# Row maxima of three attentions: from products over 128 rows, one head at a time, to products over 64 rows, two heads side by side

## The chip, the cores and the metric

The program runs on one NeuronCore of a Trainium2 chip. The core has a matrix engine (TensorE, "PE" in the profile, with "PEld" for its weight loads), three engines for elementwise work (VectorE "DVE", ScalarE "ACT", GpSimd "POOL"), and a queue engine (SyncE, "SP") that issues most transfers between the device's memory and the core's own memory (SBUF). Matrix products land in a small accumulator memory, PSUM, which DVE and ACT read. Each engine runs its own instructions in order; they wait for one another through semaphores.

The metric is the time of one execution on the device in microseconds (us). Three runs of the kernel before took 3617.41, 3617.8 and 3612.1 us; the median is 3617.41.

## The reference, cut to what matters

The program is four blocks on an input of 4 batches, 1024 positions and 128 channels. Each block normalizes x, computes an attention-like part s and a gate g from it, and adds s * g:

```
xn = _layernorm(x, axis=-1)
s = _L0_attn_ref(xn, ...)          # block 0: 16 heads of 8, window of 250, causal
g = _silu(_L0_ffn_ref(xn, ...))
x = x + s * g
```

Blocks 0, 1 and 2 hold attentions with 16 heads of dimension 8. They differ in which keys a query sees:

```
mask = (delta >= 0) & (delta < CONTEXT)   # block 0 ("window"), CONTEXT = 250
mask = jnp.tril(...)                      # block 1 ("causal")
                                          # block 2 ("full"): no mask
scores = jnp.einsum('bhtd,bhsd->bhts', q, k) * D ** (-0.5)
attn = jax.nn.softmax(scores, axis=-1)
x = jnp.einsum('bhts,bhsd->bhtd', attn, v)
```

Around them run a channel mix (block 0), a mixture of experts for all tokens (block 1), a feed-forward layer and a mixture of experts with limited places (block 2). Block 3 is a state-space layer with two layers of local attention; the change doesn't touch it.

## The kernel before, in words

**Products of parts.** q and k are computed in float32 and split into three bfloat16 parts each (`_split`, line 166), so that a float32 product becomes nine bfloat16 products of parts. With a head dimension of 8, the nine products take 72 rows of the contraction: `q9` holds the three parts of q three times over, `k9` each part of k three times (rows 0 to 71). Rows 72 to 74 of `q9` hold the three parts of the negative row maximum, and `k9` is 1 there: a product over all 128 rows is then the score less its row's maximum. The rest is zero against one.

**Units.** A unit is one batch with four of its sixteen heads: 16 units in each of the three attentions, in the order of `order` (line 516). For each unit, `load` (line 278) fetches `q9` and `k9` from the device's memory, where `project` had stored the parts (`store`, line 245): three transfers of 24 rows for q (L285), nine of 8 rows for k (L288), and, from the fourth unit on, one of zeros into rows 72 to 74 (L290), because the buffers go round and the maxima are computed with the same tile before the rows of maxima are filled. There are three pairs of buffers.

**Maxima.** `maxima(n)` (line 293) makes steps for unit n. A step takes a PSUM tile `max_ps` of two banks of 512 columns (two such tiles in rotation, shared with others), fills it with products of 128 queries of a head with the keys that they see (L317), adds the mask by a product of the identity with a mask tile (L333) for each head, and reduces it on DVE with a negated maximum (L344) into `neg`. There are 14 steps to a unit in the window stage, 22 in the causal one, 32 in the full one. `split` turns the maxima into three parts on POOL; `spread` transposes them on PE (`neg_ps`), copies them on DVE and stores them into rows 72 to 74 of `q9` by three transfers (L371, `negr`).

**Weights.** `attend(n)` (line 397) computes, for each block of keys, the transposed scores less the maxima (`sc`, L410, lhsT from `k9`, rhs from `q9`), their exponentials on ACT (L417), in blocks with a mask a select on POOL (L387), and the products with the values into `o_ps` (L438), in four column tiles of 32. In steps, `first` does two heads' scores, `second` the values of an earlier block and the other two heads' scores. There are 40 scores to a unit in the window stage, 48 in the causal one and 64 in the full one.

**Order.** `rest` (line 524) goes through the units: beside the weights of unit n run the remaining steps of the maxima of n + 1, their split, the first steps of n + 2 (two fifths of them, `lead`), and the spread of n + 1. At the start of unit n, `load(n + 2)` is issued. The streams are interleaved evenly by `_interleave` (line 174), with the projections of the next batch and parts of the neighbouring blocks among them.

```
ahead = steps[lead:] + ending[:1]
last = ending[1]
if n + 2 < N:
    load(n + 2)
    steps, ending = maxima(n + 2)
    ahead += steps[: lead - 2] + [last] + steps[lead - 2 : lead]
```

PE's instructions stay in the order in which the program records them (`keep_in_program_order`). The order on other queues, SP's among them, is set by a planner when the program is built: an instruction without a pin can stand earlier or later than in the text.

Of the kernel before, what the change touches and what calls it, by code (L numbers as in the profile page):

```python
# [185 lines left out]
def _attention(k, pool, mode, xT, w, out, rope=None):  # L186
# [9 lines left out]

    nc = k.nc
    scale = HD**-0.5
    dense = {}
    units = {}  # L200
    place = 16 * ("window", "causal", "full").index(mode)
# [76 lines left out]
    def load(n):  # L278

        b, g = order[n]  # L280
        q9, k9 = k.q9[(place + n) % 3], k.k9[(place + n) % 3]
# [7 lines left out]
        if place + n > 2:  # L289
            nc.sync.dma_start(q9[72:75].rearrange("p h t -> p (h t)"), k.zeros)  # L290
        units[n] = (q9, k9)

    def maxima(n):
# [3 lines left out]
        def tile_of(parts):  # L297


            def step():  # L300
                q9, k9 = units[n]
                if "neg" not in held:
                    held["neg"] = pool.tile([P, 4, NT], F32, tag="neg", name="neg", bufs=3)
                neg = held["neg"]
                ps = ps2("max_ps")
                flat = ps.rearrange("p a c -> p (a c)")
                _, qt0, _ = parts[0]
                lo = max(0, qt0 - 2) * P if mode == "window" else 0
                hi = T if mode == "full" else (qt0 + 1) * P
                width = hi - lo  # L310
                for j, qt, place in parts:
                    lhs = q9[:, j, qt * P : qt * P + P]
                    for c0 in range(lo, hi, 512):
                        c1 = min(c0 + 512, hi)
                        at = place + c0 - lo
                        masked = mode != "full" and c1 == hi
                        matmul(  # L317
                            flat[:, at : at + c1 - c0],
                            lhsT=lhs,
                            rhs=k9[:, j, c0:c1],  # L320
                            start=True,
                            stop=not masked,
                            skip_group_check=True,
                        )
                        if masked:
                            mw = min(c1 - c0, k.mask[mode].shape[1])

                            W = k.mask[mode].shape[1]
                            spans = [(W - P, W)]
                            if W - mw < W - CONTEXT:  # L330
                                spans.insert(0, (W - mw, W - CONTEXT))
                            for m0, m1 in spans:
                                matmul(  # L333
                                    flat[:, at + c1 - c0 - W + m0 : at + c1 - c0 - W + m1],
                                    lhsT=k.ident16,
                                    rhs=k.mask[mode][:, m0:m1],
                                    start=False,
                                    stop=m1 == W,
                                    skip_group_check=True,
                                )  # L340
                j0, m = parts[0][0], len(parts)
                stride = parts[1][2] - parts[0][2] if m > 1 else width
                of = flat[:, 0 : m * stride].rearrange("p (n c) -> p n c", n=m)[:, :, 0:width]
                nc.vector.tensor_reduce(neg[:, j0 : j0 + m, qt0], of, AX.X, ALU.max, negate=True)  # L344

            return step

        steps = []
        for qt in range(NT):
# [4 lines left out]
            for j in range(0, 4, per):  # L354
                steps.append(tile_of([(j + i, qt, i * pitch) for i in range(per)]))
# [1689 lines left out]
```

## Time and profile before

One execution was profiled. It took 3610.66 us; the span from its first to its last instruction is 3608.9 us, at a mean granted clock of TensorE of 0.951.

| what | value |
|---|---|
| the profiled execution's own time | 3610.66 us |
| its span | 3608.9 us |
| median of the three runs | 3617.41 us |
| PE busy | 3138.7 us, 87% |
| DVE busy | 2445.6 us, 68% |
| ACT busy | 1988.7 us, 55% |
| POOL busy | 1417.2 us, 39% |
| products into max_ps, masks not counted | 2198 recorded, 625.0 us busy |
| reductions of max_ps on DVE | 1088, 1177.9 us busy |
| scores of the weights on PE | 2403 recorded, 651.8 us busy |
| loads of q9 / of k9 / of zeros | 144 / 432 / 45 transfers |

How to read it: "busy" is the time in which an engine has an instruction in work, and products on PE are pipelined, so that one product's time is longer than its distance from the next; distances are read from the timeline's start times. In a line of groups stand the source line, the engine and operation, the tile written and the tiles read, the shapes, the count, the busy time, the mean duration of one in ns, and the idle time of the engine before them with what ended it. A PE shape such as 128\*128 is rows by columns of the array that the product uses. In a line of the timeline stand start and length in us, the engine, the same names and a count of merged instructions; the bracket is the engine's idle time before it and what ended it. In the trace, the window stage of block 0 lies roughly between 100 and 500 us, the causal stage of block 1 between 800 and 1300, the full stage of block 2 between 1520 and 2430, and block 3 after 2500.

### The profile page before, as it was taken

The numbers are of one execution on the slowest core, as the hardware profiler recorded it, in microseconds if no ns is written. First come the engines' busy times: TensorE is split into PE (matmuls) and PEld (weight loads), VectorE is DVE, ScalarE is ACT, GpSimd is POOL, SyncE is SP. The second block draws the span as 40 slices with busy tenths as digits, with TensorE's granted clock in tenths as the row PEclk, the third lists the DMA queues.
The fourth block names the chain that finished last, engine by engine and source line by source line (L and its number), as shares of the span: only waits on it lengthen the run. The fifth ranks groups of instructions, "written<-read, shape, count | busy, mean of one in ns | idle before, by whom it ended". The sixth has DMA issues, their size and how long they took to land. (4 is left out here: it accounts for less than half of the span.)

```text
span 3608.9 us, 64740 instructions
## 1 busy us (share of the span) xinstructions
PE 3138.7 (87%) x24592; PEld 1704.4 (47%) x24729; DVE 2445.6 (68%) x4927; ACT 1988.7 (55%) x4191; POOL 1417.2 (39%) x1962
## 2 busy tenths in 40 slices
PE   4889889999898986899999989677499999989897
PEld 3545446654343433433323333223366666666665
DVE  7667664457777752788786766652587888778785
ACT  2444453346555552366665665554366666666674
POOL 5555552012323223030321300211576667656663
PEclk8999999999999997999999999888699999999999
DMA  3322312112222102011111221100210111010110
GB/s 99 71 60 55 70 42 83 46 33 51 57 42 57 34 22 69 21 44 28 41 34 33 55 53 31 33 19 9 78 22 18 21 25 24 18 25 22 29 26 21
DMA packets 133083, 146.09 MB, mean 40 GB/s; under 512 B 80403, under 2 KB 107931, under 8 KB 125467
## 3 DMA queue, kind: packets, MB, share of 16 engines
q1 hardware_dynamic: 130724, 137.75, 16.0%
q0 software_dynamic: 2048, 4.20, 0.4%
q8 instruction: 196, 3.21, 0.4%
q14 instruction: 115, 0.93, 0.1%
HBM read 93.83 MB, written 30.11 MB: 34 GB/s over the span
## 5 line engine op out<-in xcount | busy, mean ns | idle before, releaser
L417 ACT ACTIVATE pt<-sc 128x512 f32<-128x512 f32 (+3 forms) x2432 | 1077.0, 511 | 786.1 <-PE sc L78 737.7
L344 DVE TENSOR_REDUCE neg<-max_ps 128x1 f32<-128x1024 f32 (+6 forms) x1088 | 1177.9, 1102 | 477.2 <-PE max_ps L78 424.1
L78 PE MATMUL sc<-q,k 128*128 128x512 bf16 (+3 forms) x2403 | 651.8, 342 | 126.2 <-ACT pt L417 70.0
L78 PE MATMUL max_ps<-k,q 128*128 128x512 bf16 (+3 forms) x2198 | 625.0, 350 | 86.2 <-DVE neg L344 39.5
L78 PE MATMUL o_ps<-pt,va 128*32 128x512 f32 (+3 forms) x4864 | 560.6, 527 | 19.9 <-POOL pt L387 10.2
L387 POOL TENSOR_SCALAR_AFFINE_SELECT pt<-pt 128x256 f32<-128x256 f32 (+2 forms) x768 | 292.3, 399 | 568.2 <-ACT pt L417 566.3
L78 PEld LDWEIGHTS <-k 128*128 128x128 bf16 x2432 | 183.0, 98 | 544.2 <-issue 418.1
L78 PEld LDWEIGHTS <-q 128*128 128x128 bf16 x2304 | 222.7, 99 | 359.6 <-issue 241.2
L168 POOL CAST negp<-neg 128x32 bf16<-128x32 f32 x48 | 10.2, 212 | 719.3 <-DVE neg L344 719.2
L1603 ACT ACTIVATE pr<-lsc,nb,r 128x128 f32<-128x128 f32 x512 | 202.7, 476 | 61.2 <-DVE nb L1595 57.6
L1524 POOL TENSOR_TENSOR qn<-qn,rot 128x512 f32<-128x512 f32 x128 | 164.9, 1294 | 139.8 <-DVE rot L1516 125.9
L1533 POOL TENSOR_TENSOR rn<-ss,neghalf 128x16 f32<-128x16 f32 x64 | 188.9, 2951 | 68.8 <-DVE ss L1531 59.3
L78 PEld LDWEIGHTS o_ps<-pt,va 128*32 128x32 f32 x4864 | 99.7, 109 | 213.8 <-issue 160.3
L691 ACT ACTIVATE h<-hp,eb 128x512 f32<-128x512 f32 x128 | 80.9, 684 | 197.8 <-PE hp L78 190.2
L78 PEld LDWEIGHTS <-ident 128*128 128x128 bf16 x1472 | 146.2, 100 | 87.5 <-issue 22.7
L1441 PE MATMUL qk_ps<-wqkv,hT 128*128 128x512 f32 x256 | 137.9, 623 | 24.9 <-DVE hT L1487 10.3
L78 PE MATMUL hp<-xT,ew 128*128 128x512 f32 x256 | 130.3, 634 | 19.7 <-ACT rope_t L234 9.3
L701 DVE SCALAR_TENSOR_TENSOR xn<-op,gates,xn 128x128 f32<-128x128 f32 x256 | 72.1, 344 | 100.4 <-PE op L78 100.4
L78 PEld LDWEIGHTS op<-ew,h 128*128 128x128 f32 x1024 | 123.6, 192 | 20.1 <-issue 17.0
L78 PE MATMUL max_ps<-mask_window,ident 128*128 128x134 bf16 (+2 forms) x960 | 132.0, 221 | 0.0
L78 PE MATMUL op<-ew,h 128*128 128x128 f32 x1024 | 125.3, 276 | 0.0
L65 POOL TENSOR_TENSOR ln_rs<-ln_ve,neghalf 128x4 f32<-128x4 f32 x72 | 73.7, 1025 | 113.1 <-DVE ln_ve L63 109.7
(347 smaller groups left out, 5452.9 us busy)
## 6 DMA issues: line engine op xcount, KB each, us to landing
q<-qx SPq DMA_DIRECT2D x144, 192.0 KB
k<-kx SPq DMA_DIRECT2D x432, 64.0 KB
va<-vb SPq DMA_DIRECT2D x120, 128.0 KB
x<-x SPq DMA_DIRECT2D x20, 512.0 KB
qx<-qp SPq DMA_DIRECT2D x12, 768.0 KB
kx<-kp SPq DMA_DIRECT2D x12, 768.0 KB
ew<-in_e1w_dram SPq DMA_DIRECT2D x64, 128.0 KB
x<-in_x_dram SPq DMA_DIRECT2D x8, 512.0 KB
```

The source lines that it names most:

```text
L65: nc.gpsimd.tensor_tensor(rs, ve, k.neghalf[:, :n], ALU.pow)
L78: k.tc.keep_in_program_order(k.nc.tensor.matmul(*args, **kw))
L168: eng.tensor_copy(dst[:, 0], src)
L344: nc.vector.tensor_reduce(neg[:, j0 : j0 + m, qt0], of, AX.X, ALU.max, negate=True)
L387: nc.gpsimd.affine_select(out=pt, in_=pt, pattern=[[0, 2], [step, pt.shape[2]]], compare_op=ALU.is_ge, fill=0.0, base=base, channel_multip ...
L417: nc.scalar.activation(pt[:, j % 2, :width], sc[:, :width], AF.Exp, scale=scale)
L691: nc.scalar.activation(h[:, hh, :], hp[:, hh, :], AF.Gelu, bias=eb1[:, e, hh : hh + 1])
L701: nc.vector.scalar_tensor_tensor(to, op[:, c, :], gates[:, 4 * n + c, e : e + 1], to, ALU.mult, ALU.add)
L1441: pin(nc.tensor.matmul(*args, **kw))
L1524: nc.gpsimd.tensor_tensor(qn[:, i], qn[:, i], rot, ALU.add)
L1533: nc.gpsimd.tensor_tensor(rn, ss.rearrange("p w h -> p (w h)"), k.neghalf[:, : 2 * NH], ALU.pow)
L1603: nc.scalar.activation(t.pr[:, h, :], t.sc[r][:, c, :], AF.Exp, bias=t.nb[r][:, c : c + 1], scale=t.r8[:, h : h + 1])
```

## The change

Maxima get their own operands. `load_pairs` fetches, for a unit, tiles `q8` and `k8` of 128 rows by two heads: rows 0 to 63 hold two heads of the unit, rows 64 to 127 the other two. Eight products of parts are kept (the one of the two lowest parts is left out), which fill 64 rows. A product over 64 rows then takes half of the array, and products for the two halves are recorded one behind the other, each into its own bank of the PSUM tile. The weights keep `q9` and `k9` with nine products over 128 rows.

The masks are added once per bank: one product of the identity over 128 rows with the mask repeated for all places of the bank, before the products where the mask covers a whole block of 128 keys, after them where it covers six columns. For this, window and causal maxima are taken block of keys by block of keys: the diagonal block, the one before it and the one before that in the window stage; the diagonal block, keys up to 512 and keys from 512 on in the causal one; the two halves of the keys in the full one. Each part has its own `neg`; `split` first takes the minimum of the parts on DVE.

`load(n + 1)` is now issued at the start of unit n, with two pairs of buffers in place of three, and after it `load_pairs(n + 2)`, also with two. The zeros fall away. The steps of a unit are 11, 20 and 32.

```
-        q9, k9 = k.q9[(place + n) % 3], k.k9[(place + n) % 3]
+        q9, k9 = k.q9[n % 2], k.k9[n % 2]
...
-        if place + n > 2:
-            nc.sync.dma_start(q9[72:75].rearrange("p h t -> p (h t)"), k.zeros)
...
+    def load_pairs(n):
+        b, g = order[n]
+        q8 = pool.tile([P, 2, T], BF16, tag="q8", name="q8", bufs=2)
+        k8 = pool.tile([P, 2, T], BF16, tag="k8", name="k8", bufs=2)
+        for a in range(2):
+            heads = slice(4 * g + 2 * a, 4 * g + 2 * a + 2)
+            for r in range(3):
+                r0, ns = 64 * a + 24 * r, 3 if r < 2 else 2
+                nc.sync.dma_start(q8[r0 : r0 + 8 * ns], dense["q", b][0 : 8 * ns, heads, :])
+                for s in range(ns):
+                    nc.sync.dma_start(k8[r0 + 8 * s : r0 + 8 * s + 8], dense["k", b][8 * r : 8 * r + 8, heads, :])
+        pairs[n] = q8, k8
...
+                def mask(first):
+                    m0, m1 = masked
+                    m = k.mask[mode][:, m0:m1].unsqueeze(1).to_broadcast([P, len(slots), m1 - m0])
+                    for a in range(2):
+                        to = ps[:, a, 0 : len(slots) * pitch].rearrange("p (n c) -> p n c", c=pitch)
+                        matmul(
+                            to[:, :, 0 : m1 - m0], lhsT=k.ident16, rhs=m, start=first, stop=not first, skip_group_check=True
+                        )
+                whole = masked is not None and masked[1] - masked[0] == P
+                if whole:
+                    mask(True)
+                for i, qt, c0, c1, place in slots:
+                    for a in range(2):
+                        rows = slice(64 * a, 64 * a + 64)
+                        matmul(
+                            ps[:, a, place : place + c1 - c0],
+                            lhsT=q8[rows, i, qt * P : qt * P + P],
+                            rhs=k8[rows, i, c0:c1],
+                            start=not whole,
+                            stop=whole or masked is None,
+                            skip_group_check=True,
+                        )
+                if masked is not None and not whole:
+                    mask(False)
...
+        if mode == "full":
+            steps = [step for qt in range(NT) for part in range(2) for step in spans(part, qt, 512 * part, 512 * part + 512)]
...
+        elif mode == "causal":
+            steps = tiles(0, 0, 0, (0, P))
...
+            steps = tiles(0, 0, 0, (2 * P, 3 * P)) + tiles(1, 1, 1, (P, 3 * P - CONTEXT)) + tiles(2, 2, 2, (0, P))
...
         def split():
             neg = held.pop("neg")
+            for part, first in enumerate(firsts[1:]):
+                to = neg[:, 0, :, first:]
+                nc.vector.tensor_tensor(to, to, neg[:, 1 + part, :, first:], ALU.min)
+            neg = neg[:, 0]
...
-    begin = project(0) + [lambda: load(0), lambda: load(1)] + steps + ending
+    begin = project(0) + [lambda: load_pairs(0), lambda: load(0), lambda: load_pairs(1)] + steps + ending
...
+                load(n + 1)
                 if n + 2 < N:
-                    load(n + 2)
+                    load_pairs(n + 2)
                     steps, ending = maxima(n + 2)
```

`tiles` makes steps for one part in blocks of 128 keys (eight places of 128 columns in a tile), `spans` steps for a range of up to 512 keys, one step for all four heads up to 256 keys and two above.

## The prediction

> **What bounds the kernel now.** I read the page's busy shares first, then busy time by stage, then two stretches of the timeline in the stages that the change touches.
>
> ```profile
> span 3608.9 us, 64740 instructions
> PE 3138.7 (87%) x24592; PEld 1704.4 (47%) x24729; DVE 2445.6 (68%) x4927; ACT 1988.7 (55%) x4191; POOL 1417.2 (39%) x1962
> L344 DVE TENSOR_REDUCE neg<-max_ps 128x1 f32<-128x1024 f32 (+6 forms) x1088 | 1177.9, 1102 | 477.2 <-PE max_ps L78 424.1
> L78 PE MATMUL max_ps<-k,q 128*128 128x512 bf16 (+3 forms) x2198 | 625.0, 350 | 86.2 <-DVE neg L344 39.5
> ```
>
> ```profile
> 100.00:500.00 400.00, 358.24 (x3301) 203.28 (x3299) 265.80 (x441) 193.90 (x565) 221.20 (x526) 0.97 0.30 64
> 800.00:1300.00 500.00, 458.12 (x3318) 202.13 (x3349) 367.93 (x584) 283.30 (x660) 152.06 (x308) 0.98 0.21 49
> 1570.00:2090.00 520.00, 484.45 (x2638) 169.73 (x2690) 397.48 (x493) 329.13 (x623) 119.33 (x124) 0.99 0.17 38
> ```
>
> The second fence is busy time in a stretch of the window stage (block 0), the causal stage (block 1) and the full stage (block 2): PE, PEld, DVE, ACT, POOL, then clock, DMA share, GB/s. PE is busy 90, 92 and 93%; DVE 66 to 76%. PE runs in order, so whatever its next instruction waits for delays all behind it. One block of weights in the full stage:
>
> ```profile
> 2101.37 1.07 PE L78 MATMUL o_ps<-pt,va 128*32 128x512 f32 x8
> 2102.37 0.61 PE L78 MATMUL sc<-q,k 128*128 128x512 bf16 x2
> 2102.81 0.59 PE L78 MATMUL max_ps<-k,q 128*128 128x512 bf16 x2
> 2103.24 0.64 PE L78 MATMUL sc<-q,k 128*128 128x512 bf16 x2
> 2103.72 0.38 PE L78 MATMUL max_ps<-k,q 128*128 128x512 bf16 x1
> 2104.24 1.06 PE L78 MATMUL o_ps<-pt,va 128*32 128x512 f32 x8
> ```
>
> Start to start a 512-column bf16 product takes 0.215 us (2102.37 to 2102.81 is two), so 0.42 us per 1000 columns. The last line of maxima has one record missing: two end at 2103.72 + 0.43 = 2104.15, and the 128*32 products start at 2104.24. That 0.09 is the price of changing the tile size; start times in nanoseconds give 0.093 at every such change, also from and to block 3's 64*128 products. The period is 2.87 us. Now the window stage, PE and then the queue of SP:
>
> ```profile
> 204.33 0.27 PE L78 MATMUL sc<-q,k 128*128 128x256 bf16 x1 [0.26 <-ACT pt L417]
> 205.29 0.22 PE L78 MATMUL max_ps<-k,q 128*128 128x128 bf16 x1 [0.69 <-DMA q<-zeros]
> ```
>
> ```profile
> 191.91 0.29 SPq L285 DMA_DIRECT2D q<-qx  x1
> 192.25 0.97 SPq L288 DMA_DIRECT2D k<-kx  x3
> 193.27 0.29 SPq L285 DMA_DIRECT2D q<-qx  x1
> 193.60 0.97 SPq L288 DMA_DIRECT2D k<-kx  x3
> 195.53 0.29 SPq L285 DMA_DIRECT2D q<-qx  x1
> 196.60 1.92 SPq L288 DMA_DIRECT2D k<-kx  x3
> 199.75 0.23 SPq L290 DMA_DIRECT2D q<-zeros  x1
> ...
> 210.88 1.77 SPq L371 DMA_DIRECT2D q<-negr  x3
> 215.28 0.29 SPq L285 DMA_DIRECT2D q<-qx  x1
> ```
>
> ```profile
> 191.90:204.90 13.00, 11.96 (x120) 6.63 (x118) 9.29 (x12) 7.42 (x24) 6.30 (x19) 1.00 0.52 94
> ```
>
> A unit (four heads) starts at 191.91 with the 13 loads for the unit two ahead. Eight are issued 0.34 us apart, each later one waits for the one eight places earlier, and they move at 94 GB/s (last number of the last fence). The first maxima tile that needs them waited 0.69 us, until 205.29. So transfers already touch PE's path in this unit.
>
> **The change part by part. PE.** Columns of maxima products per unit: 10752 window, 18432 causal, 32768 full, times 16 units, at 0.42: 72, 124, 220 us. Two heads side by side halve them: -36, -62, -110. That row halves do overlap is shown in block 3:
>
> ```profile
> 2805.38 0.59 PE L1441 MATMUL lsc<-mask_local,ident 128*128 128x512 bf16 x2
> 2805.90 1.21 PE L1441 MATMUL lsc<-qkT 64*64 64x64 f32 x64
> ```
>
> Sixty-four products (two f32 passes of 16 groups of two row by two column tiles) start within 1.0 us, 0.058 per group pass, where 64 columns at f32's 0.427 us per 512 are 0.053. So a group costs some 0.006 more than one product: 1600 pairs, +10, of which I count +8.
>
> The scores of the weights stay at 128 rows, and so do the masks. In the two built programs' order on PE, tile size changes 324 times against 618 in the window stage, 363 against 805 in the causal, 511 against 1322 in the full one: +294, +442, +811, at 0.093: +27, +41, +75. The Trainium skill, TensorEngine Tiling (Array Packing), Key Properties, says that changing the tiling mode, not just the tile, drains the engine; that speaks against this change and has no figure. With changes free, the saving would be the whole 208 us; by the rows it is 65.
>
> Masks keep their columns (7336 a unit in the window stage, 4096 causal) in fewer instructions: no time. Net PE: -9, -21, -35. What reaches the end: in the full stage I lay out one block with 0.093 at five changes instead of two. The fourth score would come 1.07 us after the first, but it waits for ACT to empty the first one's buffer (1.136 now: 2102.37 to 2103.50), so the block takes 2.76, not 2.69: -0.11 in some 220 blocks, **-24**. Causal, PE-bound by nine tenths less ACT's waits: **-16**. Window: half comes before the wait priced below and is lost: **-4**.
>
> **DVE.** The same elements are reduced in 11, 20 and 32 steps a unit, not 14, 22, 32; rows of 1024 take 1.22 us, with 1 or 4 outputs. 80 small minima are added; 128x32 subtractions on POOL take 0.25, so 16 us in all, beside PE, whose transpose of the maxima has 2 us or more to spare: +3.
>
> **Transfers.** The zeros go (one of 13 a unit); 22 loads of q8 and k8 come, 1 MB. In the built order of SP's queue, five or six of them stand ahead of the previous unit's negr stores (window; eight in causal, ten or more in full) and are early: they wait for nothing but the end of maxima, which lies 7 us before negr (last reduce 204.1, negr 210.88), and take 1.7 us of issue, so negr is not delayed. Then come negr, the 12 loads of the next unit, and only then the other 16 or 17 (11 causal). Maxima of the unit after next need all 22 at their first tile, at the same place in PE's order as now (after 20 to 22 of 40 scores; causal 24 of 48, was 26). The 12 loads land 12.6 us after the unit's start (12.0 to 13.9 in the trace's DMA semaphores). Those with 8 rows of 8 KB land 0.72 apart, those with 24 rows 1.45. The new ones have rows of 4 KB, no row of this trace has that shape: ends are half of these times and the 0.16 us that a 4 KB packet takes alone. I take half (same engines, same pattern): 13 x 0.36 + 4 x 0.65 = 7.3, landing at 19.9. For the first unit of a batch the stores of kx and x stand ahead: 23.5.
>
> The Trainium skill, DMA: Bandwidth & Descriptors, lets a DMA of 8 rows run on 8 of 16 engines at some 27 GiB/s each; in the trace 8 packets are indeed in flight, but at half that rate. By the page's rate the loads would land near 15.5 and the waits below would sum to an estimated 14 us; by the rows they are 42.
>
> First reduces of the twelve later window units start 15.5, 14.1, 20.1, 21.6, 19.1, 19.9, 20.1, 22.4, 18.8, 18.9, 14.8, 13.6 us after the loads' start (0.7 after the first product). Waits against 19.9 + 0.7 (23.5 + 0.7 for the first, fifth and ninth): 8.7, 6.5, 0.5, 0, 5.1, 0.7, 0.5, 0, 5.4, 1.7, 5.8, 7.0 = **+42**. Behind the waiting product stand the unit's last scores, for which ACT and POOL wait. PE idle over 2 us is followed in the trace by 3.4 us at clock 0.5, some +10; about as much is caught up, as ACT's waits shrink. Causal: deadline 17 to 28 less 1.5, landing 18: **+7**. Full: 32 or later: 0. The 12 loads of the next unit lose their third buffer: they were wanted 14 us after their issue, now a unit after it (23 us or more), so they cost nothing themselves; all their price is that the 17 stand behind them.
>
> Sum: window +38, causal -9, full -24, minima +3, pairs +8: **+16**. The profiled execution took 3610.66 (span 3608.9 and 1.8 around it), 6.75 below the median of 3617.41; on the median that is 3633.
>
> **Rivals.** *Loads in time (the other side).* If the 17 late loads land 0.2 us apart, they are down by 12.6 + 3.4 = 16.0 (19.6 for a batch's first), the same sum of waits gives 15, a third of it caught up: 10; causal none. Then 10 - 4 - 16 - 24 + 11 = -23, 3594. The sign changes near 18.2, which is 0.33 us per load, between the ends above (I took 0.43 on the mean). For it, 4 KB packets alone move at full rate; against it, the 0.69 us wait with only 13 loads. *Pairs overlap in part.* If weight loads of the two halves queue, or bf16 pairs cost 0.05 more, 1600 pairs add 80: 3700. Block 3 shows f32 alone. *No overlap*: +208 on PE, some 3800; block 3 speaks against it. *Nothing moves* (within 0.2%, 7 us, about what a measurement here can tell): waits near 30.
>
> **How the numbers follow.** Waits as priced or longer 0.44, in time 0.30, partial overlap 0.09, none 0.03, even 0.14. Faster 0.30, same 0.14, slower 0.56. The range runs from full-stage gains of -34 with hardly a wait (3580) to loads that take 0.6 each (waits near 80) or a partial overlap: 3700.
>
> **What would show it.** Pairs of 64*128 products start 0.01 us apart and 0.22 us per pair; 0.09 at each change; a block of 2.76 us in the full stage; in the window stage PE waits for DMA k<-kx or q<-qx at a unit's first maxima tile, units of 30 to 34 us where they had 23 to 33, fewer digits of 9 for PE there. Wrong if the window stage keeps its length, or if the full stage doesn't get shorter.

## The result, and the profile after

The kernel after took 3649.47 us (median of four runs, 3640.26 to 3667.34) against 3614.76 us for the kernel before (four runs). The ratio is 1.0105, with a 95% interval of 1.0061 to 1.0149: slower by about 1%. The forecast was slower, 3633 us, in a range of 3580 to 3700: its direction and its range held, but the medians lie 35 us apart where the sum had +16. The profiled execution has a span of 3652.5 us where before it was 3608.9; all times by stage, here and in the experiments, are of one profiled execution of each kernel.

The lines of the page that answer to those shown of before:

```profile
span 3652.5 us, 66473 instructions
PE 3134.7 (86%) x24953; PEld 1549.4 (42%) x24953; DVE 2456.4 (67%) x4926; ACT 1987.5 (54%) x4189; POOL 1415.2 (39%) x1961
L356 DVE TENSOR_REDUCE neg<-max_ps 128x2 f32<-128x1024 f32 (+2 forms) x1008 | 1165.4, 1178 | 487.2 <-PE max_ps L78 480.8
L78 PE MATMUL max_ps<-k,q 64*128 64x128 bf16 (+2 forms) x3520 | 406.1, 296 | 109.1 <-DVE neg L356 52.3
```

The products of maxima keep PE busy for 406 us instead of 625, yet PE's whole busy time falls by 4 us only. Where it went is seen by stage. I take a stage from the start of its first exponential on ACT to the end of its last one; PE's idle time and the time at half clock are summed over the same stretch, from PE's instructions and from the trace's clock records.

| stage | before | after | difference | predicted | PE idle | at half clock |
|---|---|---|---|---|---|---|
| window | 444.8 | 491.5 | +46.7 | +38 | 49.9 to 87.2 | 34.1 to 81.9 |
| causal | 582.2 | 573.1 | -9.1 | -9 | 54.2 to 60.2 | 27.3 to 47.8 |
| full | 975.6 | 975.5 | -0.1 | -24 | 115.8 to 127.7 | 62.7 to 103.2 |
| all the rest | 1606.3 | 1612.4 | +6.1 | 0 | | |

(The sum of the prediction had 11 us more, for minima and pairs, that it gave to no stage.) So the causal stage came out as forecast, the window stage somewhat longer, and the full stage did not get shorter at all.

Stretches of the three stages after, by engine as before (PE, PEld, DVE, ACT, POOL, then clock, DMA share, GB/s). They lie at the same work only roughly; what is to be seen is the clock, 0.92, 0.96 and 0.96 where it was 0.97, 0.98 and 0.99 before, and the traffic, 90, 77 and 56 GB/s where it was 64, 49 and 38:

```profile
100.00:500.00 400.00, 331.17 (x3160) 148.50 (x3158) 249.51 (x397) 175.12 (x513) 205.61 (x481) 0.92 0.39 90
850.00:1350.00 500.00, 450.24 (x3402) 154.19 (x3399) 378.58 (x589) 288.20 (x671) 153.06 (x313) 0.96 0.33 77
1600.00:2120.00 520.00, 482.36 (x2679) 136.38 (x2678) 400.79 (x509) 330.38 (x625) 118.85 (x124) 0.96 0.23 56
```

One block of the full stage, PE's timeline: from 1811.73 to 1814.49 it lasts 2.76 us, as the prediction laid it out (2.87 before). A score of 512 columns and the pair behind it start 0.31 apart, 0.22 of columns and 0.09 of the change:

```profile
1811.73 1.07 PE L78 MATMUL o_ps<-pt,va 128*32 128x512 f32 x8
1812.73 0.60 PE L78 MATMUL sc<-q,k 128*128 128x512 bf16 x2
1813.27 0.39 PE L78 MATMUL max_ps<-k,q 64*128 64x512 bf16 x2
1813.59 0.65 PE L78 MATMUL sc<-q,k 128*128 128x512 bf16 x2
1814.17 0.39 PE L78 MATMUL max_ps<-k,q 64*128 64x512 bf16 x2
1814.49 1.07 PE L78 MATMUL o_ps<-pt,va 128*32 128x512 f32 x8
```

The two products of a pair start 0.003 us apart in the trace's start times, and from pair to pair it is 0.055 to 0.067 us for 128 columns and 0.226 for 512, where before the change one score of 512 columns followed the other after 0.215 to 0.227: the halves overlap fully.

The window stage, SP's queue and PE in one unit. The 12 loads of the next unit (q, L286, and k, L289) stand first, the late part of q8 (L301) and k8 (L303) behind them. The second of the two issues at 212.53 is the last that PE's next maxima need (it lands at 215.96; the issues from 213.27 on are for the unit after). These maxima wait twice:

```profile
196.31 0.29 SPq L286 DMA_DIRECT2D q<-qx  x1
...
200.94 2.08 SPq L289 DMA_DIRECT2D k<-kx  x3
204.16 1.84 SPq L303 DMA_DIRECT2D k<-kx  x3
...
212.53 0.65 SPq L303 DMA_DIRECT2D k<-kx  x2
```

```profile
211.35 0.21 PE L78 MATMUL max_ps<-k,q 64*128 64x128 bf16 x1 [1.55 <-DMA q<-qx]
216.16 0.58 PE L78 MATMUL max_ps<-k,q 64*128 64x128 bf16 x7 [4.59 <-DMA q<-qx]
```

What PE waited for in the window stage (total us, times, longest), after and then one line of before:

```profile
PE ot L82 <- DVE os L491: 18.7, 14, 3.2
PE max_ps L78 <- DMA k<-kx: 15.8, 8, 4.3
PE max_ps L78 <- DMA q<-qx: 12.5, 4, 4.6
```

```profile
PE ot L82 <- DVE os L448: 5.4, 5, 2.3
```

So 28.3 us are waits for the new loads. Another 13 come from a wait that I had not priced: the transposes of the weighted values wait for DVE's copy of `o_ps`.

The full stage. In its tenth unit, which begins at 2056.0, PE, SP and POOL show this:

```profile
2071.56 1.30 PE L82 MATMUL tr_ps<-ident,slots_tm 128*128 128x128 f32 x5 [4.68 <-DMA slots_tm<-sent]
```

```profile
2064.37 2.85 SPq L303 DMA_DIRECT2D k<-kx  x3
...
2068.80 0.93 SPq L1105 DMA_DIRECT2D slots_tm<-sent  x2
2069.83 0.37 SPq L250 DMA_DIRECT2D qx<-qp  x1
```

```profile
2074.54 1.04 POOL L168 CAST kp<-kd 128x1024 bf16<-128x1024 f32 x1 [12.16 <-DMA qx<-qp]
```

The load of `slots_tm`, which belongs to block 2's mixture of experts, was issued 12.8 us after the unit's start, behind loads of k8. Before the change it was issued at 2017.75, 8.6 us ahead of the unit's start at 2026.3. The store of the next batch's q parts is as late, and POOL waits 12.16 us for it. This unit takes 70.2 us, 60.8 before.

In the fourteenth unit, PE and ACT:

```profile
2390.69 0.61 PE L78 MATMUL sc<-q,k 128*128 128x512 bf16 x1 [17.29 <-DVE at L504]
2406.70 0.58 PE L78 MATMUL sc<-q,k 128*128 128x512 bf16 x1 [15.40 <-ACT pt L460]
```

```profile
2376.47 1.06 ACT L697 ACTIVATE xn<-xn 128x1024 f32<-128x1024 f32 x1 [0.72 <-POOL xn L87]
2403.68 1.06 ACT L697 ACTIVATE xn<-xn 128x1024 f32<-128x1024 f32 x1 [26.15 <-POOL xn L87]
```

L697 is the activation of a batch's gate. In the built order of the kernel before, eight exponentials stand between the second and the third of these in the full stage; in the kernel after none does. So ACT waits 26 us for the rows of the third gate, with the exponentials for which PE waits queued behind it. Before the change PE's first wait was there too (16.6 us); the second was 7.25 us.

### The profile page after: what moved, and what is told of

It reads as the page before. It is cut to its first block, busy times and chain, and to the rows that moved or that the text cites. A ratio compares the mean times of both kernels' runs of the same rounds, so it can differ in the third digit from the quotient of the medians.

```text
span 3652.5 us, 66473 instructions
## 1 busy us (share of the span) xinstructions
PE 3134.7 (86%) x24953; PEld 1549.4 (42%) x24953; DVE 2456.4 (67%) x4926; ACT 1987.5 (54%) x4189; POOL 1415.2 (39%) x1961
## 3 DMA queue, kind: packets, MB, share of 16 engines
q1 hardware_dynamic: 152720, 186.99, 20.9%
## 5 line engine op out<-in xcount | busy, mean ns | idle before, releaser
L356 DVE TENSOR_REDUCE neg<-max_ps 128x2 f32<-128x1024 f32 (+2 forms) x1008 | 1165.4, 1178 | 487.2 <-PE max_ps L78 480.8
L78 PE MATMUL sc<-q,k 128*128 128x512 bf16 (+3 forms) x2432 | 668.6, 349 | 111.4 <-ACT pt L460 82.1
L78 PE MATMUL max_ps<-k,q 64*128 64x128 bf16 (+2 forms) x3520 | 406.1, 296 | 109.1 <-DVE neg L356 52.3
L78 PEld LDWEIGHTS <-k 128*128 128x128 bf16 x2432 | 154.3, 98 | 564.4 <-issue 499.9
L78 PEld LDWEIGHTS <-q 64*128 64x128 bf16 x3520 | 139.8, 96 | 552.7 <-issue 487.0
L1483 PE MATMUL qk_ps<-wqkv,hT 128*128 128x512 f32 x256 | 137.5, 621 | 24.7 <-DVE hT L1529 10.3
L78 PE MATMUL hp<-xT,ew 128*128 128x512 f32 x256 | 135.5, 658 | 20.2 <-DVE neg L356 11.4
L1634 DVE TENSOR_REDUCE top<-lsc 128x4 f32<-128x512 f32 x128 | 82.5, 683 | 43.0 <-PE lsc L1483 42.8
L491 DVE COPY os<-o_ps 128x512 f32<-128x512 f32 x96 | 65.6, 683 | 55.5 <-PE o_ps L78 55.4
```

The source lines that it names most:

```text
L78: k.tc.keep_in_program_order(k.nc.tensor.matmul(*args, **kw))
L356: nc.vector.tensor_reduce(to, of, AX.X, ALU.max, negate=True)
L1483: pin(nc.tensor.matmul(*args, **kw))
L1634: nc.vector.tensor_reduce(top, t.sc[r], AX.X, ALU.max)
```

## The experiments

The planner orders each queue anew at every edit, even where the edit touches neither the engine nor the block. The first runs showed this, and later ones hold part of the order. All ratios are to the kernel before, run on the same chip in the same set.

**Pairs first.**

```
-                load(n + 1)
                 if n + 2 < N:
                     load_pairs(n + 2)
+                load(n + 1)
+                if n + 2 < N:
```

> The 22 loads of q8 and k8 stand ahead of the 12 loads of the next unit's q9 and k9; nothing else is edited. Theory of late loads: the pairs land some 12 to 13 us after the unit's first load instead of 19 to 21, the first maxima tile comes at 18 to 20, so PE's waits there (28.3 us in the window stage after the change) and the stretches at half clock behind them go; window stage 491.5 us to 440 to 450. The built order on ACT also puts the second of the two activations of the gate in the full stage 22 exponentials behind the first, where it stood 8 behind it before the change and directly behind it after; if that place costs the full stage its gain, it falls from 975.5 to some 960 us. Total near 3595. Rival, PE's work: the changes of tile size and the pairs make the window stage long by themselves: it stays within 8 us of 491, total near 3640. Rival, the full stage is bound by other engines: it stays within 3 us of 975.5.

Measured: 1.0141 (1.0116 to 1.0166), no gain at all. Window 473.0, causal 611.5, full 945.0. PE's waits in the window stage for loads into maxima fell from 28.3 to 7.9 us, as expected, but the time did not come out. What PE waited for, in the window and in the causal stage, and SP in the causal one:

```profile
PE max_ps L78 <- DVE neg L356: 20.9, 3, 10.3
```

```profile
PE sc L78 <- DMA q<-negr: 42.2, 5, 11.5
```

```profile
873.56 0.51 SPq L414 DMA_DIRECT2D q<-negr  x1
884.77 0.39 SPq L250 DMA_DIRECT2D kx<-kp  x1
885.21 1.89 SPq L414 DMA_DIRECT2D q<-negr  x2
```

The planner had put the store of the next batch's k between the first and the second store of `negr`. That store waits for POOL's split of k, so two rows of maxima left 11 us late and the scores waited for them. On DVE it had put the 26 instructions of a layer norm in one piece between two reductions (before and after the change they stand in four pieces), which made the waits of 10.3 us. The full stage did get shorter, by 30 us, with the third gate 22 exponentials behind the second. The window stage is above the 440 to 450 that was expected, and the causal one 38 us longer than in the kernel after. Both rivals fall, and the theory stands only in part: a wait was removed and the order of other work changed with it.

**No loads of pairs after the first two units.**

```
     def load_pairs(n):
+        if n > 1:
+            pairs[n] = pairs[n - 2]
+            return
```

> Left out: the loads of q8 and k8 of all but the first two units of each attention; the later units compute their maxima from those of the first two. So 42 units have 12 loads in place of 34. Theory of late loads: the window stage is that of no wait at all, 436 to 446 us (before 444.8); the causal stage, where no load was waited for, keeps its 573 within 5; the full stage loses the 4.7 us wait for slots_tm in its tenth unit, which stood behind stores and loads in the queue, and has the activations of the gate 22 exponentials apart: 955 to 963. Total near 3585. Rival, PE's work or the half clock that comes with products over 64 rows: window above 480 and the half clock stays at some 80 us there.

Measured: 0.9978 (0.9965 to 0.9991). Window 460.9, causal 593.2, full 936.0. There is no wait for these loads, but the same piece of layer norm on DVE costs 20.9 us in the window stage again, and the causal stage has waits of 13.9, 13.7 and 5.8 us at scores, most of it for `negr`; the full stage is shorter than the 955 to 963 expected. The tenth unit of the full stage takes 60.6 us, as before the change: its 9.4 us came from the loads.

**Products over 128 rows in place of pairs.**

```
-                            lhsT=q8[rows, i, qt * P : qt * P + P],
-                            rhs=k8[rows, i, c0:c1],
+                            lhsT=q8[:, i, qt * P : qt * P + P],
+                            rhs=k8[:, i, c0:c1],
```

> The products of maxima read all 128 rows instead of 64, so each one uses the whole array, no two overlap and the tile size doesn't change between maxima and scores (324, 336 and 537 changes where there were 618, 805 and 1322); what is computed is left wrong in one part: a product adds up the scores of two heads, so the maxima are of sums. Everything else (tiles, masks, loads, reductions) is as after the change. By the terms of the prediction PE gets 36, 62 and 110 us of columns back and gives up 27, 44 and 73 of changes: the full stage is longer by 24 us (block of 2.87 in place of 2.76), the causal by 12 to 18, the window stage, which waits for loads, by 0 to 6: total near 3692. If pairs overlap less than block 3 showed, the difference is smaller: nothing at 0.05 us more for a pair. If products over 64 rows bring the half clock, its time falls from 82, 48 and 103 us to the 34, 27 and 63 of before.

Measured: 1.0199 (1.0175 to 1.0222). Here the built orders of PE, ACT and POOL are those of the kernel after and DVE's and SP's differ in a handful of places, so the stages compare directly: window 482.3 (-9.2), causal 584.5 (+11.4), full 995.5 (+20.0). Full and causal are near what the terms give, so pairs minus changes are worth about what was predicted. The window stage got shorter, with more work on PE: the time at half clock fell to 61.4, 34.1 and 87.0 us from 81.9, 47.8 and 103.2, part of the way to before.

**Fewer, larger loads.**

```
-                for s in range(ns):
-                    nc.sync.dma_start(k8[r0 + 8 * s : r0 + 8 * s + 8], dense["k", b][8 * r : 8 * r + 8, heads, :])
+                of = dense["k", b][8 * r : 8 * r + 8, heads, :].unsqueeze(0).to_broadcast([ns, 8, 2, T])
+                nc.sync.dma_start(k8[r0 : r0 + 8 * ns], of)
```

> Each part of k8 comes by one load of 24 (or 16) rows with the source repeated, in place of three (or two) of 8 rows: 12 loads of pairs for a unit where there were 22, the same bytes. By the prediction's prices (0.65 us for 24 rows of 4 KB, 0.36 for 8), the late part of them is some 2 us shorter, so PE's waits of 28.3 us in the window stage fall to some 10 and the stage to 470 to 480; causal and full as after the change, total near 3635. Rival, bytes set the landing: the window stage stays at 488 to 495. Rival, each load costs by its number (0.7 us each however large): late loads halve, window 450 to 460, total near 3610.

Measured: 1.0089 (1.0065 to 1.0113). Window 492.0, with 31.3 us of waits for these loads: 12 loads for a unit take as long as 22. So the bytes and not their number set the landing, as the first rival said. (The full stage, 947.9, again had another place for the gates: its last four units take 252.0 us instead of 266.4. The other 13 us that it is shorter were not traced.)

**The order held.** Four kernels in which the exponentials, the gates, the loads and the stores of `negr` stay in the order in which the program records them, so that ACT's order is the same in all of them, but for the kernels' own differences:

```
-                    nc.scalar.activation(pt[:, j % 2, :width], sc[:, :width], AF.Exp, scale=scale)
+                    k.tc.keep_in_program_order(nc.scalar.activation(pt[:, j % 2, :width], sc[:, :width], AF.Exp, scale=scale))
...
-            nc.sync.dma_start(q9[rows], dense["q", b][:, heads, :])
+            k.tc.keep_in_program_order(nc.sync.dma_start(q9[rows], dense["q", b][:, heads, :]))
```

and likewise for the other loads, `negr` and the gates. In the third the pairs come first, and the store of k moves to the start of a batch's third unit:

```
-                streams.append((coming[:3], coming[3:7], coming[7:])[g])
+                streams.append((coming[:3], coming[3:6], coming[7:])[g])
...
+            if b + 1 < B and g == 2:
+                coming[6]()
```

> The kernel before, with the exponentials and the gates' activations on ACT and the loads of q9 and k9 and the stores of negr on SP held in the order in which the program records them; the planner still places the rest. In the full stage the gates' second and third activations now stand 64 and 128 exponentials behind the one before, in the same places as in the other three kernels of this set, so that full stages can be compared without the planner's choice. Theory that the place of those activations took the full stage's gain: its thirteenth and fourteenth unit (76.7 and 77.6 us) change by several us, whatever the maxima do; window 445 and causal 582 stay within 5 and 10 us. Rival (the place does not matter): all three stages as before within 5 us.

> The kernel after, with the same instructions held in recorded order (loads of q8 and k8 too: none is hoisted ahead of negr any more, so the 12 loads of q9 and k9 come first and all 22 behind them). Against the same kernel without the change: full stage shorter by the 24 us of the prediction, less up to 9 where the queue's loads hold up slots_tm; if PE's saving does not reach the end there, 0 within 5. Causal shorter by 5 to 12. Window longer by 45 to 70: all 22 loads are now late, some 2 us a unit more than in the kernel after (landing near 22 in place of 19 to 21).

> As the run with the same order held, but the 22 loads of q8 and k8 are recorded ahead of the 12 of q9 and k9, and the store of the next batch's k stands at the start of the third unit of a batch instead of within the second, so that no store stands ahead of negr. The layer norms on DVE stand between reductions in four pieces, as before and after the change, not in one piece as in the first run with pairs first. Theory of late loads and of the planner's order: no wait of 10 us for a reduction and none of 11 us for negr any more; window 440 to 455, causal 560 to 575, full 5 to 10 us on either side of the run with the loads of q9 and k9 first; total 3560 to 3590, faster than both kernels. Rival, PE's work makes the window stage long: window above 470.

> Left out, as in the earlier run without them: the loads of q8 and k8 of all but the first two units of each attention; the rest is as in the run of the kernel after with the order held, layer norms on DVE in four pieces. It bounds what the loads cost by any route. Theory of late loads: window 432 to 445, causal 560 to 573, full shorter by 5 to 10 us than with the loads (no wait for slots_tm). If more than 15 us of the window stage's lengthening stay (above 460), the loads are not the main cause.

| order held | ratio (interval) | window | causal | full | at half clock (window, causal, full) |
|---|---|---|---|---|---|
| before | 0.9991 (0.9981 to 1.0001) | 441.2 | 576.6 | 966.2 | 34.1, 20.5, 44.6 |
| after | 1.0243 (1.0222 to 1.0263) | 508.1 | 616.4 | 956.7 | 102.4, 85.3, 79.5 |
| after, pairs first | 1.0043 (1.0026 to 1.0060) | 469.0 | 580.4 | 964.6 | 85.3, 51.2, 79.4 |
| after, no pair loads | 0.9920 (0.9904 to 0.9937) | 449.4 | 577.8 | 940.8 | 44.4, 51.2, 72.9 |

In the second of them, with all 22 loads late, PE waited in the window stage and (last line) in the causal one

```profile
PE max_ps L78 <- DMA k<-kx: 41.4, 14, 4.7
PE max_ps L78 <- DMA q<-qx: 10.3, 5, 4.0
```

```profile
PE max_ps L78 <- DMA k<-kx: 32.8, 13, 4.4
```

Several expectations failed here. With all loads late the causal stage is 39.8 us longer than before, where 5 to 12 us shorter was expected: its maxima wait for the loads too. With the pairs first the window stage is 469.0 in place of 440 to 455, and the program is slower than the kernel before, not faster. Without the loads the window stage is 4 us above its range. And held order alone makes the three stages of the kernel before 18.6 us shorter but not the program, because 22 us more stand outside of them.

What follows. Of the 66.9 us by which the window stage is longer with the order held, 58.7 go when the loads go: the loads are the main cause, as predicted. The 8.2 that stay are 18.4 us more of PE's idle time (47.8 to 66.2: the copy of `o_ps` is waited for 22.7 us and a reduction behind a layer norm 13.6) less 10.2 of its busy time. Ordering the pairs first wins 39 of the 59. PE's idle time is then that of the run without loads (66.8 and 66.2 us), and the other 20 us answer to the clock: 85.3 us at half clock against 44.4, of which half the difference is lost. The full stage without pair loads is 25.4 us shorter than before; with them it is shorter by 9.5 or 1.6 only. But not all of the 16 to 24 us between these runs is the price of the loads. PE waited for reductions in this stage, before with the order held and then without pair loads:

```profile
PE max_ps L78 <- DVE neg L344: 31.2, 19, 9.4
```

```profile
PE max_ps L78 <- DVE neg L359: 20.3, 21, 6.8
```

The longest of the first line, 9.4 us in the thirteenth unit, comes from a layer norm that stands in DVE's queue ahead of the reduction and waits for POOL. The run of the kernel after with the order held has it too (9.2 us); in the build without pair loads the planner set that layer norm three reductions later, and the wait is gone. What is shown of the loads' own price in this stage is the wait for `slots_tm`, 9.4 us with the pairs first. The causal expectation of the last run (560 to 573) failed: the store of k stands ahead of `negr` in that build, and two waits of 14.2 us came back at scores.

**The gates alone.** The kernel after with only exponentials and gates held; the orders of SP and POOL are those of the kernel after to within a few instructions.

```
-        lambda a=slice(b * NT, b * NT + NT): k.nc.scalar.activation(g[:, a, :], g[:, a, :], AF.Silu)
+        lambda a=slice(b * NT, b * NT + NT): k.tc.keep_in_program_order(
+            k.nc.scalar.activation(g[:, a, :], g[:, a, :], AF.Silu)
+        )
```

> The kernel after with one thing held: on ACT, exponentials and the gates' activations stay in recorded order, so that in the full stage the second and third gate stand 64 and 128 exponentials behind the one before instead of 68 and none. SP's and POOL's orders are those of the kernel after. Theory that two gates together on ACT took part of the full stage's gain: its last four units (266.4 us after) fall to some 257, as in the run with SP's order held too, the full stage to 966, window 492 and causal 573 within 5 us; total near 3640. Rival, the gates' place is of no account: full within 3 us of 975.5. What then still stands between 966 and the 951 of the prediction is the tenth unit's wait behind the loads (9.4 us).

Measured: 1.0050 (1.0031 to 1.0070); window 484.4, causal 572.2, full 954.4. The full stage is 21.1 us shorter than in the kernel after, 18.4 of it in the last four units, more than expected. The tenth unit stays at 70.3 us. So the place of two activations on ACT, which the diff doesn't touch, is worth about half of the whole slowdown against the kernel before as it stands. (The planner moved 90 instructions on DVE with it, in ten places, all in the last units of this stage; the share of these is not known.) In the kernel before these activations stand badly too: held there together with the loads, the same stage is 9.4 us shorter. With the gates held in both kernels the full stage is 11.8 us shorter by the change, and the tenth unit still takes 9.5 back.

**Scores over 64 rows.**

```
-                        lhsT=k9[:, j, kt * P : kt * P + P],
-                        rhs=q9[:, j, c0 : c0 + width],
+                        lhsT=k9[0:64, j, kt * P : kt * P + P],
+                        rhs=q9[0:64, j, c0 : c0 + width],
```

> As the run of the kernel after with the order held, but the products of scores read rows 0 to 63 of q9 and k9 alone, in tiles of 64 rows, so that the tile size doesn't change between maxima and scores (818 changes in the full stage where there were 1322, 612 against 805 in the causal, 737 against 618 in the window stage, where masks and maxima still differ). Left out: the ninth product of parts and the subtraction of the maxima in the scores. Theory that each change costs PE 0.093 us: full stage, 504 fewer, 47 us less on PE; ACT's own pace (a block cannot be shorter than its fourth score's wait for ACT, 1.14 us after the first) lets some 20 to 30 of it reach the end: 927 to 937 in place of 957. Rival, the changes are hidden behind ACT: within 5 us of 957. Window, bound by loads, and causal: within 10 us of 508 and 616.

Measured: 1.0294 (1.0273 to 1.0316). Full 937.8, 18.9 us shorter than with the order held, just short of the range expected: of the 47 us that 504 changes cost PE, some two fifths reach the end, with 22 us more at half clock against them. The causal stage, 615.3, is as expected. But the window stage went to 543.7, outside of what I expected, with less idle time (82.2 us against 101.0) and 213.6 us at half clock against 102.4.

**Half the rows in the kernel before.**

```
-                    lhs = q9[:, j, qt * P : qt * P + P]
+                    lhs = q9[0:64, j, qt * P : qt * P + P]
...
-                            rhs=k9[:, j, c0:c1],
+                            rhs=k9[0:64, j, c0:c1],
```

and the same for masks and scores.

> The kernel before with the order held, whose products of maxima, masks and scores read rows 0 to 63 alone, one product after the other; loads, columns and orders stay. Left out: the ninth product of parts, the subtraction of the maxima in the scores and half of the mask's rows in the maxima. It asks whether products over half the rows bring more time at half clock by themselves: with scores over 64 rows the window stage had 214 us at half clock with 82 us of PE idle, where the run with the same order and scores over 128 rows had 102 with 101. Tile size changes 487 times in the window stage in place of 324, which is 15 us on PE. If rows count for the clock: half clock in the window stage above 100 us where the run before with the order held had 34, window 441 to some 490. If only idle time counts: half clock 30 to 45 us, window 450 to 460.

Measured: 1.1183 (1.1121 to 1.1245). Window 515.6, causal 709.6, full 1141.1, with 225.4, 355.0 and 479.2 us at half clock. One stretch of it, and the same stretch of the kernel before with the order held (columns as in the stretches above):

```profile
300.00:400.00 100.00, 98.66 (x545) 48.82 (x543) 45.29 (x98) 33.90 (x97) 31.62 (x85) 0.50 0.16 36
```

```profile
300.00:400.00 100.00, 88.80 (x794) 49.39 (x793) 64.34 (x108) 45.77 (x136) 55.23 (x126) 0.95 0.25 54
```

PE is busy for 98.66 of 100 us and the granted clock stays at 0.50. By idle time alone the clock should have come back; of the two expectations, the one in which rows count holds, and by more than the 490 us that it gave for the window stage. The changes of tile size do not explain it: the kernel after has more of them in this stage (618 against 487), and there no stretch at half clock is longer than 6.8 us, where here one is 119.5 us.

**A version from the parts.** Block 0 computes its maxima as before, blocks 1 and 2 as after, block 2 with its pairs first:

```
+    paired = mode in ('causal', 'full')
+    maxima = maxima_64 if paired else maxima_128
...
+                if mode == "full" and n + 2 < N:
+                    load_pairs(n + 2)
+                if paired:
+                    load(n + 1)
```

> A version put together from what the runs showed: block 0 computes its maxima as the kernel before does (products over 128 rows from q9 and k9, three pairs of buffers, zeros), blocks 1 and 2 as the kernel after does; in block 2 the loads of q8 and k8 are recorded ahead of those of q9 and k9, and its gate's activations on ACT stand as in the first run with pairs first. If the stages add up as they were seen one by one (window 445, causal 573, full 945 us, the rest as before), the span is some 3609 + 0 - 9 - 31 = 3569, 1.1% faster than the kernel before. If the window stage of the kernel after had been long for another reason than its own maxima and their loads, it stays above 470 and the total near 3600.

Measured: 3596.86 us, 0.9967 (0.9955 to 0.9980): faster than both kernels, by a third of a per cent against before. Window 444.0 and full 949.4 add up as expected, so the window stage is long through its own maxima and their loads. The causal stage kept 582.3, without the 9 us; the tenth unit of the full stage has 71.9 us still. The span is 3593.2 us where the sum of the parts gave 3569: 9 us of that are the causal stage, 4 the full one, and 11 stand outside of the three stages, where I had expected nothing. How much of the full stage's 26 us the gates' place would give the kernel before alone was not tried without holding loads too.

## Why the prediction was right, and where it was not

**PE's own work: right.** Pairs overlap, a change of tile size is 0.09 us, the full stage's block is 2.76 us. In the trace of before, scores of 512 columns follow one another after 0.215 to 0.227 us at full clock and after 0.40 to 0.43 at half, so PE's work takes about twice as long there. PE was busy at half clock for 32.0, 21.6 and 31.9 us before and 68.0, 39.4 and 49.5 after. Its busy time less half of these fell by an estimated 9, 24 and 21 us in the three stages (by 10, 24 and 31 between the two kernels with the order held), where I had 9, 21 and 35. The rivals of partial or no overlap fall.

**Loads in the window stage: right in kind.** The last load that a unit's maxima need was issued 14.7 to 18.3 us after the unit's first one, and the first reduction came 18.1 to 22.5 us after it, around the 19.9 + 0.7 that I had. PE's waits for them are 28.3 us, not 42; the +38 was nearly met by luck, because two terms that I had set too small came in. PE was busy at half clock for 36.0 us more, which costs about 18 where I counted 10 and had as much caught up again; and the wait for the copy of `o_ps` grew by 13 us, for which I had no term. In sum, 9 us less of PE's work, 18 more for the clock and 37 more of idle time make the +47. The rival that the loads come in time falls.

**Full stage, -24: the step that failed, on the way to the end.** The block is as short as forecast, and in the first nine units 10.7 us were saved. Two things took it back. First, "Full: 32 or later: 0": I asked when q8 and k8 are wanted and not who stands behind them in SP's queue. `slots_tm` and the store of q stood behind them, 9.4 us in the tenth unit. Second, the planner put two gates together on ACT, and the last four units are 4.9 us longer than before instead of shorter; I had followed the built order of PE and SP and not that of ACT. The mechanism itself was right: with the orders of PE, ACT and POOL unchanged, products over 128 rows make the stage 20.0 us longer again. That the saving is 25.4 us with the loads out and the gates held is in part luck: PE's work is 35 us less, the clock takes 15 of that back, for which the forecast of this stage had no term, and PE is idle for 6 us less, because the wait behind the layer norm is gone. By the prediction's own sign ("if the full stage doesn't get shorter") this part was wrong.

**Causal, -9: met by luck, from other terms.** The +7 of waits for loads did not come: no maxima of this stage waited for a load of q8 or k8. PE's saving of some 24 us lost about 9 to the clock and 6 to idle time, for a reduction or the copy of `o_ps`.

**Minima, masks and the extra pair cost** are too small to be told apart here. The stages' surroundings, counted as nothing, gave +6.1: between window and causal stage 7 us more, where 56 loads for the first units now stand instead of 26; no run took this apart. So the kernel is slower for the reason named, the loads, and for one not named, the order that the planner gave to other work.

**Small slips in the working.** Half of 1.45 is 0.73 and not 0.65, which puts the landing at 20.2; against a landing at 15.5 the waits sum to 12 and not 14; the pairs are 1760 (3520 recorded products) and not 1600; 80 minima of 0.25 us are 20 and not 16 us (one of 128x32 takes 0.19 in the runs). None of these changes the forecast by more than about 4 us.

## What to carry to other kernels

Where a planner sets the order, an edit moves work on engines that it doesn't touch: compare the built order of every queue, and hold the order in both kernels before asking what an edit is worth. A load's price is not only when its data is wanted but also what waits behind it in an in-order queue; here that was 9.4 us in the full stage, where no maxima waited for the loads. Products over half of the rows can bring the half clock, alone far more than in pairs, and the clock should be read before the saving is believed.

## What the runs showed of the hardware

The granted clock does not follow PE's busy time alone. With products over 128 rows, half clock comes in pieces of 3.4 us, mostly after a piece in which PE was idle for some 1.7 us or more, and mostly ends after one or two pieces. With the same columns over 64 rows it stayed at 0.50 for up to 55 such pieces (188 us) on end, once for 75 us without any idle time of PE, and the program took 12% longer. The Trainium skill, "TensorE: Matmul & The Clock Gate", Part 1, says that about 3.4 us of sustained busy time bring the full clock back; for products over 128 rows the traces agree, for products over 64 rows alone the run above shows otherwise. In the kernel after, where two halves run side by side between products over 128 rows, half clock is 0.94, 0.79 and 0.81 of PE's idle time by stage, against 0.68, 0.50 and 0.54 before, and 0.80, 0.55 and 0.65 in the run with products over 128 rows in place of pairs. The halves have a part in this. Of the pieces of 3.4 us at full clock in which PE was idle for 1.4 to 1.8 us, 4 of 25 were followed by half clock in the three stages of the runs without halves (before, before with the order held, 128 rows in place of pairs), and 64 of 115 in the eight runs with pairs and scores over 128 rows; above 2 us it was 45 of 46 and 149 of 149. The way in which the idle time is spread has a part too: with the order held, the window stage fell to half clock 13 times with the pairs first and 6 times without their loads, at 66.8 and 66.2 us of idle time.

For loads of 4 KB rows, the number of transfers did not matter: 12 or 22 transfers of the same 1 MB left the window stage at 492.0 and 491.5 us.
